# Storing the ranked mask rows seven steps after their gather, from eleven buffers, in a four-layer graph attention kernel

## The chip, the cores and the metric

The kernel runs on one core of a Trainium2 chip. The metric is device time in microseconds (us), the median of several executions. Times inside an execution come from one profiled execution; they are counted from the start of its span.

## What is computed

There are 3,327 nodes with 512 features, a 0/1 adjacency matrix with few ones, and four graph attention layers of 8, 4, 1 and 8 heads. Each layer normalises the features, projects them, and gives every node the softmax-weighted mean of its neighbours' projected rows. The layers follow one another, so no node of a layer can be finished before the rows of its neighbours from the layer before exist:

```python
h = jnp.maximum(_layernorm(x, axis=-1), 0.0)
x = x + _L0_gnn_ref(h, adj, L0_gnn_W, L0_gnn_a_src, L0_gnn_a_dst)
h = jnp.maximum(_layernorm(x, axis=-1), 0.0)
x = x + _L1_gnn_ref(h, adj, L1_gnn_W, L1_gnn_a_l, L1_gnn_a_r)
...
```

Within a layer (here layer 1):

```python
e = jax.nn.leaky_relu(sl[:, :, None] + sr.T[None, :, :], negative_slope=NEG_SLOPE)
e = jnp.where(mask[:, None, :], e, -jnp.inf)
alpha = jnp.nan_to_num(jax.nn.softmax(e, axis=2), nan=0.0)
out = jnp.einsum('nhm,mhd->nhd', alpha, Wh).reshape(n, OUT_DIM)
```

## The kernel before

**Lists.** A first stage turns the adjacency matrix into lists of neighbours and ranks the nodes by how many neighbours they have, so that tile 0 holds the 128 nodes with the longest lists and tile 25 those with the shortest (`CAPS`, from 36 slots down to 11). All of it is 26 tiles of 128 nodes. After that the kernel works in rank order.

**Layers.** A layer reads a table of projected rows in device memory (`tabx` in layer 0, then `tabs[1]` and `tabs[0]` in turn; the page names them all `tab`) and writes the next table. `Tile` handles one tile: `fetch` (line 856) issues from GpSimd (POOL) one indirect gather of 128 rows per list slot, four slots to a buffer `g`; `scored` (875) makes the softmax weights; `group` (897) multiplies the rows with their weights on VectorE (line 916) and adds them up on TensorE (line 921). When a tile's last group is done, `finish` and `ends` (1004, 994) place what follows some steps later: the means, the normalisation, four transposes (450), the projection (468), the scaling of the new rows `v` on ScalarE (475), and the store of the tile's 128 new rows into the next table on SyncE's DMA queue (SP), line 992. In layers 1, 2 and 3 the tiles with the longest lists (one tile, nine tiles, two tiles: `DENSE`) are not gathered but computed as whole masked rows by `Several` and `Wholes`.

**Masks.** The masks for those whole rows are made in layer 0. `Mask` gathers adjacency rows, turns them, and stores the result in `found` by columns in the old node order. `Ranked` (1050) brings them into rank order: for each of the 26 row tiles, its `fetch` gathers 128 rows of 288 int32 from `found` on POOL and stores them into `masks` on SP (line 1060). Between the two the rows lie in one of three buffers inside the tile `spare`. `Ranked`'s `scored`, `group` and `finish` do nothing.

**Order of the work.** Line 1389 runs over the steps of a layer. Each step issues the fetches of steps up to `LOOK` = 7 ahead, then the pieces placed by `later` (335), then the `scored` of the next step and the `group` of this one. In layer 0 the list of steps ends like this (lines 1381 and 1382), with tile 0's groups last among the tiles' and 18 steps that have nothing but a `Ranked`:

```python
steps[-8:] = [s for i, step in enumerate(steps[-8:]) for s in (step, (Ranked(i), 0))]
steps += [(Ranked(j), 0) for j in range(8, NT)]
```

The instructions of POOL, PE, DVE and ACT are issued in exactly the order of the code (`manual_schedule`, line 1339). SP is not in that list: the order of its queue is chosen by the scheduler of the language, which keeps to the data dependencies and may move a transfer of SP ahead of or behind others. Each transfer in the queue waits there for its own semaphores.

**The start of layer 1.** `Several.place` (1317) for tile 0 puts loads of layer 1 at its start: `s` (1221), the first slices of table rows `v` (1243) and of masks (1244), all into the tile `low`. POOL's gathers of layer 1 (834, into `g`, from `tab`) need every row of the new table, so they wait for the last store of line 992, which is tile 0's. The weights of layer 3 are loaded in the same place on SP (393), since the weights of layer 0's projection have had their last reader then.

Of the kernel before, what the change touches and what calls it, by code (L numbers as in the profile page):

```python
# [13 lines left out]
I32 = mybir.dt.int32  # L14
# [4 lines left out]
P = 128  # L19
# [18 lines left out]
ND = max(DENSE)  # L38
# [485 lines left out]
def tile_gat_stack(ctx: ExitStack, tc: tile.TileContext, x, adj, adjT, ws, avs, out):  # L524
# [266 lines left out]
    with cond.Else():  # L791
        tile_gat_lists(tc, x, adj, ws, avs, out, ident, half, slots, L, low, spare, tabx, tabs)
# [3 lines left out]
def tile_gat_lists(ctx: ExitStack, tc: tile.TileContext, x, adj, ws, avs, out, ident, half, slots, L, low, spare, tabx, tabs):  # L796
# [7 lines left out]
    nc = tc.nc  # L804
# [17 lines left out]
    wide = 3 * P  # L822

    found = dram.tile([NP, ND * P // 4], I32, name="found")
    masks = dram.tile([ND // 3, NT, P, wide // 4], I32, name="masks")
# [5 lines left out]
    L, low, spare = [t.rearrange("p a b -> p (a b)") for t in (L, low, spare)]  # L831

    def gather(out_, table, which):
        nc.gpsimd.indirect_dma_start(out=out_, out_offset=None, in_=table,  # L834
                                     in_offset=bass.IndirectOffsetOnAxis(ap=which, axis=0))
# [9 lines left out]
    class Tile:  # L845
# [10 lines left out]
        def fetch(self):  # L856

            l, t = self.l, self.t
            i = len(self.groups)
            k0 = self.k0[i]  # L860
            n = (self.k0 + [CAPS[t]])[i + 1] - k0
            g = gpool.tile([P, GROUP, ROW], F32, name="g")
            for q in range(n):
                if l > 0 and k0 + q == 0:
                    nc.sync.dma_start(g[:, 0, :], tabs[l % 2][t * P:(t + 1) * P, :])
                elif l > 0:
                    gather(g[:, q, :], tabs[l % 2], slots(t, k0 + q))
                elif k0 + q == self.own:
                    gather(g[:, q:q + 2, :].rearrange("p q n -> p (q n)"), tabx, slots(t, 0))
                else:  # L870
                    gather(g[:, q, :], tabx.rearrange("r (s n) -> (r s) n", s=2),
                           slots(t, k0 + q + (k0 == 0), twice=True))
            self.groups.append((k0, n, g))
# [23 lines left out]
        def group(self, i):  # L897


            H, K, wt = HEADS[self.l], CAPS[self.t], self.wt  # L900
            D = F // H
            k0, n, g = self.groups[i]
            if H == 1:
                for q in range(n):
                    v = g[:, q, :].rearrange("p (s m) -> p s m", s=2)[:, :, :F // 2]
                    acc = self.po.rearrange("p (s m) -> p s m", s=2)
                    w = wt[:, k0 + q, 0:1]
                    if k0 + q == 0:
                        nc.vector.tensor_scalar(acc, v, w, None, OP.mult)
                    else:  # L910
                        nc.vector.scalar_tensor_tensor(acc, v, w, acc, OP.mult, OP.add)  # L911
                return
            m = pools["m"].tile([P, GROUP, F], F32, name="m")
            for q in range(n):
                v = g[:, q, :].rearrange("p (s m) -> p s m", s=2)[:, :, :F // 2]
                nc.vector.tensor_tensor(m[:, q, :].rearrange("p (s h d) -> p s h d", s=2, d=D),  # L916
                                        v.rearrange("p s (h d) -> p s h d", d=D),
                                        wt[:, k0 + q, :H].rearrange("p (s h) -> p s h", s=2)
                                        .unsqueeze(3).to_broadcast([P, 2, H // 2, D]), OP.mult)
            for q in range(n):  # L920
                nc.tensor.matmul(self.po, ident, m[:, q, :], start=(k0 + q == 0), stop=(k0 + q == K - 1))  # L921
# [128 lines left out]
    class Ranked:  # L1050
# [3 lines left out]
            self.j, self.k0 = j, [0]  # L1054

        def fetch(self):
            n = ND * P // 4
            rows = spare[:, self.j % 3 * n:(self.j % 3 + 1) * n].bitcast(I32)
            gather(rows, found, slots(self.j, 0))
            nc.sync.dma_start(masks[:, self.j, :, :].rearrange("s p c -> p s c"),  # L1060
                              rows.rearrange("p (s c) -> p s c", c=wide // 4))

        def scored(self, i):
            pass

        group = finish = scored

    class Whole(Tile):

# [275 lines left out]
    for l in range(NL):  # L1345
# [3 lines left out]
        with ExitStack() as c2:  # L1349
# [39 lines left out]
            for s in range(-1, at_end):  # L1389
# [10 lines left out]
                if 0 <= s < len(steps):  # L1400
                    tl, i = steps[s]
# [55 lines left out]
```

## Time and profile before

| | us |
|---|---|
| median of 3 runs | 2471.52 |
| lowest and highest run | 2468.46 and 2473.81 |
| the profiled execution's own time | 3002.17 |
| its span | 3000.4 |
| layer 0's gathers end (last gather into `g`, POOL) | 1070.57 |
| layer 0's last new rows are made (ACT, start of line 475) | 1107.97 |
| layer 1's gathers begin (POOL) | 1117.48 |
| busy: PE, DVE, POOL, ACT | 2240.5, 1911.3, 1749.3, 913.9 |

A profile line of the timeline gives the start, the length, the engine, the line of the code, the operation, and what it writes from what it reads; in brackets stands how long the engine was idle before it and what ended that. SPq and POOLq are the queues in which SyncE and GpSimd issue transfers: the length there is that of the issue, not that of the transfer.

### The profile page before, as it was taken

The numbers are of one execution on the slowest core, as the hardware profiler recorded it, in microseconds if no ns is written. First come the engines' busy times: TensorE is split into PE (matmuls) and PEld (weight loads), VectorE is DVE, ScalarE is ACT, GpSimd is POOL, SyncE is SP. The second block draws the span as 40 slices with busy tenths as digits, with TensorE's granted clock in tenths as the row PEclk, the third lists the DMA queues.
The fourth block names the chain that finished last, engine by engine and source line by source line (L and its number), as shares of the span: only waits on it lengthen the run. The fifth ranks groups of instructions, "written<-read, shape, count | busy, mean of one in ns | idle before, by whom it ended". The sixth has DMA issues, their size and how long they took to land. (4 is left out here: it accounts for less than half of the span.)

```text
span 3000.4 us, 26820 instructions
## 1 busy us (share of the span) xinstructions
PE 2240.5 (75%) x6832; PEld 1225.4 (41%) x6832; DVE 1911.3 (64%) x5004; ACT 913.9 (30%) x2506; POOL 1749.3 (58%) x1739
## 2 busy tenths in 40 slices
PE   4777677777767756778778787679796677888787
PEld 2664243443334333444434344345354343444443
DVE  7887656655555545557665564697887456666655
ACT  5782122322221112323232222343333223332220
POOL 7894455565556646454556562676663556565654
PEclk9888888998899888889988888899898788898988
DMA  6885576786676677666766663787784667676664
GB/s 232 309 294 162 163 221 200 212 253 205 189 206 192 199 186 209 181 177 179 200 183 196 181 186 105 236 247 229 218 253 123 202 187 206 182 202 192 202 171 122
DMA packets 262490, 599.55 MB, mean 200 GB/s; under 512 B 103923, under 2 KB 121331, under 8 KB 257974
## 3 DMA queue, kind: packets, MB, share of 16 engines
q0 software_dynamic: 126128, 438.08, 49.7%
q1 hardware_dynamic: 132454, 152.86, 16.1%
q10 hardware_dynamic: 3744, 6.82, 0.7%
q8 instruction: 55, 0.90, 0.1%
q14 instruction: 109, 0.89, 0.1%
HBM read 547.96 MB, written 49.65 MB: 199 GB/s over the span
## 5 line engine op out<-in xcount | busy, mean ns | idle before, releaser
L921 PE MATMUL bank<-m,ident 128*128 128x512 f32 x2608 | 1328.8, 657 | 376.6 <-DVE m L916 218.1
L916 DVE TENSOR_TENSOR m<-g,pw 128x512 f32<-128x512 f32 x1304 | 811.1, 682 | 539.0 <-ACT pw L890 254.4
L834 POOL DMA_INDIRECT g<-tab,idxb x734 | 698.5, 952 | 482.2 <-issue 200.9
L921 PEld LDWEIGHTS bank<-m,ident 128*128 128x128 f32 x2608 | 528.0, 210 | 1038.3 <-issue 646.6
L468 PE MATMUL pv<-w,hT 128*128 128x264 f32 x1664 | 437.7, 418 | 80.0 <-ACT hT L457 45.5
L834 POOL DMA_INDIRECT g<-tabx,twiceb x342 | 324.2, 948 | 248.4 <-issue 153.7
L834 POOL DMA_INDIRECT g<-tab,idxa x297 | 283.0, 953 | 231.1 <-issue 95.6
L468 PEld LDWEIGHTS pv<-w,hT 128*128 128x128 f32 x1664 | 335.9, 206 | 182.5 <-ACT hT L457 52.3
L890 ACT ACTIVATE pw<-z 128x32 f32<-128x32 f32 (+4 forms) x362 | 69.1, 191 | 801.6 <-DVE z L889 442.5
L1146 PE MATMUL whole<-ve,em 128*128 128x512 f32 x468 | 230.1, 644 | 52.0 <-issue 21.8
L694 POOL TENSOR_TENSOR key<-a,keys 128x3328 int32<-128x3328 int32 (+1 forms) x29 | 189.4, 6534 | 16.2 <-DVE cand L703 12.6
L911 DVE SCALAR_TENSOR_TENSOR bank<-g,L,bank 128x512 f32<-128x512 f32 x243 | 183.3, 754 | 11.8 <-remote 3.9
L1146 PEld LDWEIGHTS whole<-ve,em 128*128 128x128 f32 x468 | 94.2, 207 | 164.7 <-issue 124.3
L834 POOL DMA_INDIRECT g<-tabx,twicea x99 | 94.4, 954 | 105.6 <-issue 55.5
L703 DVE MAX8 cand<-key 128x8 f32<-128x208 int32 x416 | 143.9, 364 | 0.1
L450 PE MATMUL pt<-ident,xn 128*128 128x128 f32 x416 | 71.4, 300 | 95.6 <-ACT xn L966 48.4
L475 ACT ACTIVATE v<-pv,rstd 128x528 f32<-128x528 f32 x78 | 54.1, 694 | 265.9 <-remote 118.6
L1271 ACT ACTIVATE spare<-room,low 128x64 f32<-128x64 f32 x208 | 57.9, 337 | 191.7 <-remote 82.2
L450 PEld LDWEIGHTS pt<-ident,xn 128*128 128x128 f32 x416 | 55.6, 155 | 137.8 <-ACT xn L966 54.9
L887 DVE TENSOR_TENSOR z<-g,pw 128x32 f32<-128x32 f32 (+4 forms) x362 | 63.1, 174 | 73.2 <-DMA g<-tab,idxa 43.3
L457 ACT ACTIVATE hT<-pt 128x512 f32<-128x512 f32 x104 | 61.4, 590 | 153.8 <-remote 85.1
L1260 ACT ACTIVATE r<-low,spare 128x256 f32<-128x256 f32 x208 | 98.9, 476 | 10.2 <-remote 2.3
(180 smaller groups left out, 2189.4 us busy)
## 6 DMA issues: line engine op xcount, KB each, us to landing
a<-in_adj SPq DMA_DIRECT2D x25, 1664.0 KB
tab<-v SPq DMA_DIRECT2D x78, 264.0 KB
ve<-tab SPq DMA_DIRECT2D x78, 264.0 KB
g<-tab SPq DMA_DIRECT2D x66, 264.0 KB
tabx<-vx SPq DMA_DIRECT2D x26, 528.0 KB
g<-tab,idxb POOLq DMA_INDIRECT x734
low<-tab SPq DMA_DIRECT2D x52, 132.0 KB
room<-tab SPq DMA_DIRECT2D x52, 132.0 KB
```

The costliest lines, as they stand in the source:

```text
L450: nc.tensor.transpose(pt[:, k, :], xn[:, k * P:(k + 1) * P], ident)
L468: nc.tensor.matmul(pv[:, s, :HF + 8], hT[:, k, :], W.w[:, k, s, :], start=(k == 0), stop=(k == KC - 1))
L694: nc.gpsimd.tensor_tensor(key[:, c:c + quarter], a[:, c:c + quarter], keys[:, c:c + quarter], OP.mult)
L703: nc.vector.max(cand[:, g * 8:(g + 1) * 8], key[:, g * SEG:(g + 1) * SEG])
L834: nc.gpsimd.indirect_dma_start(out=out_, out_offset=None, in_=table, in_offset=bass.IndirectOffsetOnAxis(ap=which, axis=0))
L887: nc.vector.tensor_tensor(z, g[:, :n, ROW - 8:ROW - 8 + H], self.s.unsqueeze(1).to_broadcast([P, n, H]), OP.add)
L890: nc.scalar.activation(self.wt[:, k0:k0 + n, :H], z, AF.Exp)
L911: nc.vector.scalar_tensor_tensor(acc, v, w, acc, OP.mult, OP.add)
L916: nc.vector.tensor_tensor(m[:, q, :].rearrange("p (s h d) -> p s h d", s=2, d=D), v.rearrange("p s (h d) -> p s h d", d=D), wt[:, k0 + q, ...
L921: nc.tensor.matmul(self.po, ident, m[:, q, :], start=(k0 + q == 0), stop=(k0 + q == K - 1))
L1146: nc.tensor.matmul(tl.po.rearrange("p (s m) -> p s m", s=2), e[:, q * P:(q + 1) * P], v.rearrange("p (s m) -> p s m", s=2)[:, :, :F // 2], ...
L1260: nc.scalar.activation(self.r[:, h, :], self.a[:, g, :], AF.Relu, bias=-1.0, scale=self.b[:, j, g:g + 1])
```

## The change

`Ranked.fetch` only gathers now. The store into `masks` is issued in `Ranked.group`, which the loop calls when the step itself is reached, seven steps (`LOOK`) after its fetch. The rows lie in `low` and no longer in `spare`; `low` has 26 x 128 = 3,328 columns, so `many` is 3328 // 288 = 11 buffers in place of three.

```diff
         def fetch(self):
-            n = ND * P // 4
-            rows = spare[:, self.j % 3 * n:(self.j % 3 + 1) * n].bitcast(I32)
-            gather(rows, found, slots(self.j, 0))
-            nc.sync.dma_start(masks[:, self.j, :, :].rearrange("s p c -> p s c"),
-                              rows.rearrange("p (s c) -> p s c", c=wide // 4))
+            n, many = ND * P // 4, low.shape[1] // (ND * P // 4)
+            i = self.j % many
+            self.rows = low[:, i * n:(i + 1) * n].bitcast(I32)
+            gather(self.rows, found, slots(self.j, 0))
 
         def scored(self, i):
             pass
 
-        group = finish = scored
+        finish = scored
+
+        def group(self, i):
+
+            nc.sync.dma_start(masks[:, self.j, :, :].rearrange("s p c -> p s c"),
+                              self.rows.rearrange("p (s c) -> p s c", c=wide // 4))
```

## Prediction

> **What bounds the kernel now.** I begin with the page: how long the span is, and what the chain of work that ended last consists of.
>
> ```profile
> span 3000.4 us, 26820 instructions
> PE 11%; DVE 7%; issue 7%; POOL 3%; ACT 2%; another core or an unknown queue 2%; DMA 1%; DVEq 0%; POOLq 0%; ACTq 0%
> ```
>
> No engine carries the whole; the four layers run one after another, each on its own mixture of gathers, DVE and PE. The change touches one place, the seam between layer 0 and layer 1. The chain view has no piece there, so I follow it by hand in the timelines, backwards from layer 1's first work. DVE first:
>
> ```profile
> 1104.09 0.15 DVE L885 COPY pw<-g 128x4 f32<-128x4 f32 x1
> 1123.85 0.17 DVE L887 TENSOR_TENSOR z<-g,pw 128x16 f32<-128x16 f32 x1 [19.61 <-DMA g<-tab,idxa]
> ```
>
> DVE has nothing to do for 19.61 us and waits for layer 1's first gathers. POOL issues them:
>
> ```profile
> 1070.57 0.94 POOL L834 DMA_INDIRECT g<-tabx,twiceb  x1 [4.21 <-issue]
> 1071.81 0.95 POOL L834 DMA_INDIRECT spare<-found,idxb  x1 [0.31 <-issue]
> 1073.06 0.95 POOL L834 DMA_INDIRECT spare<-found,idxb  x1 [0.30 <-issue]
> ...
> 1100.94 0.94 POOL L834 DMA_INDIRECT spare<-found,idxa  x1 [1.95 <-DMA masks<-spare]
> 1102.41 0.94 POOL L834 DMA_INDIRECT spare<-found,idxa  x1 [0.53 <-issue]
> 1103.82 0.94 POOL L834 DMA_INDIRECT spare<-found,idxa  x1 [0.46 <-issue]
> 1106.91 0.94 POOL L834 DMA_INDIRECT spare<-found,idxa  x1 [2.15 <-DMA masks<-spare]
> 1108.28 0.94 POOL L834 DMA_INDIRECT spare<-found,idxa  x1 [0.43 <-issue]
> 1117.48 0.94 POOL L834 DMA_INDIRECT g<-tab,idxa  x1 [8.26 <-DMA tab<-v]
> ```
>
> The first one, at 1117.48, waited for the transfer tab<-v, tile 0's new rows. Before it stand the mask gathers: the one of row tile 7 at 1071.81, that of row tile 25 at 1108.28, so 18 intervals in 36.47 us, 2.03 us each. Every third waits for a store of `masks`: three buffers hold them back. Now ACT, which makes the new rows, and SP's queue, which stores them:
>
> ```profile
> 1107.97 0.70 ACT L475 ACTIVATE v<-pv,rstd 128x528 f32<-128x528 f32 x1 [5.32 <-PE pv L468]
> ```
>
> ```profile
> 1110.52 0.39 SPq L1244 DMA_DIRECT2D spare<-masks  x1
> 1111.14 0.36 SPq L1060 DMA_DIRECT2D masks<-spare  x1
> 1111.59 0.44 SPq L393 DMA_DIRECT2D w<-in_w  x1
> 1112.08 0.53 SPq L992 DMA_DIRECT2D tab<-v  x1
> 1112.66 0.42 SPq L393 DMA_DIRECT2D w<-in_w  x1
> 1116.73 0.33 SPq L1221 DMA_DIRECT2D low<-tab  x1
> ```
>
> The rows are ready at 1107.97 + 0.70 = 1108.67, yet their store is issued at 1112.08, 3.41 us later. In front of it in the queue stand the last mask store (1111.14), which had to wait for the gather of 1108.28, and half of layer 3's weights (1111.59). The seam is therefore set by the mask rows, and only just: they end some 3 us after the computation of tile 0, which has run since 1070.57 beside them.
>
> **What the Trainium skill says.** In "DMA: Bandwidth & Descriptors", section "Anatomy of one DMA — SWDGE (gpsimd) path", it says that DMA engines do not wait on semaphores, the wait happens on the issuing sequencer before dispatch. So a store that waits for its gather holds up everything behind it in SP's queue; the 3.41 us agree. The same section prices a transfer at 2.0 us plus bytes / 436e3; for 128 x 288 x 4 = 147,456 bytes that is an estimate of 2.3 us. The trace is longer: 1106.91 to the dependent store at 1109.99 is 3.1 us, and the slowest I found (1075.69 to 1079.81) 4.1 us; I use the trace. The section "Queues, rings and completion order" of that page says that a DMA engine consumes one ring in order, so the rows' transfer also stands behind the weights' bytes issued before it on SP. The trace agrees in one comparison. At the next such seam, from layer 2 to layer 3, no weights go ahead:
>
> ```profile
> 2320.07 0.32 SPq L992 DMA_DIRECT2D tab<-v  x1
> ...
> 2323.18 1.00 POOL L834 DMA_INDIRECT g<-tab,idxa  x1 [9.77 <-issue]
> ```
>
> From the issue of the store to the first gather it is 3.1 us there, and 1117.48 - 1112.08 = 5.4 us here.
>
> **The change part by part.** It removes no instruction and adds none: 26 gathers and 26 stores remain, 147,456 bytes each.
>
> Eleven buffers: gather j now waits for store j - 11 in place of j - 3. Gathers 7 to 25 can follow at the pace of back-to-back issues on POOL, 1071.81 to 1073.06 = 1.25 us. Gather 25 is then issued at 1071.81 + 18 x 1.25 = 1094.3 instead of 1108.28. Its store, 3.1 to 4.1 us later, is issued by 1098.4. The stores of eleven back are long done: gather 22 (1090.6) needs store 11 (gather 1076.8, store by 1080.9, landed at most 3.8 us later, as store 1079.81 released the gather at 1083.62). Bytes: 2 x 147,456 per 1.25 us is 236 GB/s; between 1090 and 1105 the DMA engines moved 151 GB/s at a busy share of 0.56, so about 270 GB/s at full share in this mixture. It fits, at a share near 0.87.
>
> The delay: in the code the last new row would come before the last 13 stores. In the built instruction order of the changed kernel it does not: SP's scheduler puts all 26 stores, then tile 25's own row for layer 1, three mask loads, two table loads and the first half of the weights ahead of it. So the delay as such does nothing for that row; what helps is that the 26 stores end early. Those five loads and the tile's row stood among the stores before; at 0.45 us an issue they take 2.7 us, from 1098.4 to 1101.1. The row's store also has a semaphore wait for the transfer eight back on SP, store 25: landed by 1098.4 + 3.8 = 1102.2. SP is then idle until the weights' buffer and the rows are ready. Slack: 1108.67 - 1102.2 = 6.5 us.
>
> Moved as well: tile 1's row, at 1082.85 before, stands behind store 15 now, some 1085.4 (gather 15 at 1081.8 plus 3.6). Only a table load 15 us later reads it. An early load of layer 3's mask moves up behind store 0 and holds SP until that has landed; before, a mask load of layer 1 did the same at 1029.78. Cost nothing both times, since store 1 was not due before 1033.73. If its gather came sooner, it costs what is missing, 3.8 us at most, with 75 us of cover behind it.
>
> `low` is also layer 1's work space, so its first ACT, DVE and PE instructions, and the loads into it, wait for the mask stores to have read it. All are done by 1102.2, and layer 1's first such writer (L1236) ran at 1120.60. Nothing, as long as the 6.5 us of slack stand. `spare` becomes free earlier; nobody waits for it.
>
> The sum: the rows' store is issued when they are ready, at about 1108.75 instead of 1112.08: 3.3 us. Its way to the first gather took 5.4 us with the weights' first half 0.5 us ahead. In the changed order that half waits for PE alone: at the earliest for the first eight matmuls of the projection, which fill about half of 1102.70 to 1107.93, at the latest for its end at 1107.93. It is ahead by 0.8 to 3.4 us; the 5.4 us become something between 5.4 and 3.1. I take 1.1 us off, half the distance, so 4.4 us in all, 3.3 to 5.6. What is late next is tile 0's own computation (projection and ACT), untouched. After the seam everything hangs on those rows, so the gain is carried to the end: 3002.17 - 4.4 = 2997.8 in the profiled execution.
>
> The timed executions take 2471.52, 0.823 of the profiled one's 3002.17, and I don't know how the two chains that race here (18 mask rounds in 39.3 us, 1071.81 to 1111.14; computation of tile 0 in 38.1 us, 1070.57 to 1108.67) stand there. If both shrink alike, the gain is 4.4 x 0.823 = 3.6 us: 2467.9.
>
> **Rivals.**
> Forecast: 2467.9, 0.15% less. For it speak the waits above; chance 0.50, of which 0.10 beyond 0.2%.
> Hidden: in the timed executions the mask rounds are shorter by more than the computation. 3.4 us of 39.3 are enough, 9%, and SP is free before the rows are ready already; the gain is nil: 2471.5. For it speaks that the profiled execution is slower overall by far more than 9%, against it that nothing shows which of the two shrinks. Chance 0.18, 0.02 of it slower.
> Larger: the computation shrinks more than the rounds. In the profile SP would be free at 1102.2, so 1112.08 - 1102.2 = 9.9 us could be saved, with 1.1 for the weights 11.0, times 0.823 = 9.1: 2462.4 at the end. Midway between this and the forecast: 2465.2. Chance 0.20.
> Slower: the mask traffic does not become faster, because gathers and stores, closer together, slow each other down. Now six transfers, 2.7 us, and the wait for store 25's landing stand between it and the rows. With the old pace of 2.03 us the store is issued at 1111.14, landed at 1114.9: the rows go 2.9 us later, times 0.823 = 2.4: 2473.9. It decides once store 25 is issued after 1112.08 - 3.8 = 1108.3, its gather after 1104.7, a pace over (1104.7 - 1071.8) / 18 = 1.83 us. Against it speaks the DMA share of 0.56. Chance 0.12, of which 0.05 beyond 0.2%.
>
> **How the numbers follow.** A measurement of this kernel can tell about 0.2%, 4.9 us, from no change. Faster: 0.10 + 0.20 = 0.30; slower: 0.02 + 0.05 = 0.07; within: 0.63. The range goes from the larger gain's end, 2462.5, to the slower rival's 2474.
>
> **What would show it.** In the profile of the changed kernel: mask gathers from 1071.8 on 1.25 us apart with no wait for `masks`; the last mask store before 1100; L992's last store within 0.2 us of the end of ACT L475; the first gather from `tab` 4 to 5.6 us earlier relative to that of tile 0's last gather from `tabx`. I am wrong if the mask gathers still stand 1.8 us apart or more, if the store waits for store 25, or if the gap between ACT and the store is gone and the median has not moved.

## The result and the profile after

| | before, us | changed, us |
|---|---|---|
| median of 6 runs | 2470.99 | 2459.62 |
| lowest and highest run | 2468.46 and 2473.81 | 2455.74 and 2461.02 |
| ratio of the changed kernel to the one before, 95% interval | | 0.9951 (0.9940 to 0.9961) |
| the profiled execution's own time and its span | 3002.17 and 3000.4 | 2458.72 and 2456.9 |

The changed kernel takes 11.4 us less. The forecast was 3.6 us less, and 2459.62 lies below the whole range, whose lower end was 2462.5.

The page of the changed kernel, the line with its span:

```profile
span 2456.9 us, 26822 instructions
```

The span is 543.5 us shorter than the 3000.4 of before, while the medians differ by 11.4. The profile of before was one unusually long execution: profiled again, the same kernel took 2467.62 us with a span of 2465.9. The mean clock granted to TensorE was 0.874 in the long execution, and 0.946 and 0.947 in the profiles of after and of before taken again; what made the long one long was not found. From here on the second profile of before is the one to compare with, since it and the profile of after stand for the timed runs.

First the kernel before, profiled again, at the seam between layer 0 and layer 1. POOL's timeline, with the last gather of layer 0, the mask gathers of row tiles 7, 18, 21 and 25, and the first gather of layer 1:

```profile
887.27 0.95 POOL L834 DMA_INDIRECT g<-tabx,twiceb  x1 [0.30 <-issue]
888.52 0.95 POOL L834 DMA_INDIRECT spare<-found,idxb  x1 [0.30 <-issue]
...
914.01 0.94 POOL L834 DMA_INDIRECT spare<-found,idxa  x1 [2.02 <-DMA masks<-spare]
...
919.82 0.95 POOL L834 DMA_INDIRECT spare<-found,idxa  x1 [1.89 <-DMA masks<-spare]
...
927.13 0.94 POOL L834 DMA_INDIRECT spare<-found,idxa  x1 [0.56 <-issue]
...
936.09 0.94 POOL L834 DMA_INDIRECT g<-tab,idxa  x1 [8.02 <-DMA tab<-v]
```

ACT, which makes the new rows, and SP's queue, which stores them, in the same execution:

```profile
908.36 0.70 ACT L475 ACTIVATE v<-pv,rstd 128x528 f32<-128x528 f32 x1 [5.60 <-PE pv L468]
```

```profile
929.97 0.36 SPq L1060 DMA_DIRECT2D masks<-spare  x1
930.42 0.44 SPq L393 DMA_DIRECT2D w<-in_w  x1
930.91 0.53 SPq L992 DMA_DIRECT2D tab<-v  x1
```

The rows are ready at 908.36 + 0.70 = 909.06 and are stored at 930.91, 21.9 us later. In the long execution that gap was 3.4 us. The last mask store, at 929.97, goes out just before it, with only half of the weights between them.

Now the changed kernel, the same three views:

```profile
886.35 0.95 POOL L834 DMA_INDIRECT g<-tabx,twiceb  x1 [0.30 <-issue]
887.60 0.94 POOL L834 DMA_INDIRECT low<-found,idxb  x1 [0.30 <-issue]
...
910.12 0.95 POOL L834 DMA_INDIRECT low<-found,idxa  x1 [0.30 <-issue]
923.54 0.95 POOL L834 DMA_INDIRECT g<-tab,idxa  x1 [12.47 <-DMA tab<-v]
```

```profile
906.12 0.70 ACT L475 ACTIVATE v<-pv,rstd 128x528 f32<-128x528 f32 x1 [5.61 <-PE pv L468]
```

```profile
914.07 0.36 SPq L1069 DMA_DIRECT2D masks<-low  x1
...
917.44 0.38 SPq L393 DMA_DIRECT2D w<-in_w  x1
917.92 0.45 SPq L992 DMA_DIRECT2D tab<-v  x1
```

No mask gather waits for a store any more: the gathers of row tiles 7 to 25 take 910.12 - 887.60 = 22.5 us in place of 927.13 - 888.52 = 38.6 us. But the row is still late. It is ready at 906.82 and stored at 917.92, 11.1 us later, because the last mask store (914.07), six loads (914.52 to 917.34) and half of the weights (917.44) stand before it in SP's queue. So the same thing bounds the seam before and after the change, for less time.

I call "seam" the time from layer 0's last gather to layer 1's first: 936.09 - 887.27 = 48.8 us before, 923.54 - 886.35 = 37.2 us after. It is 11.6 us shorter, and the medians differ by 11.4. The gain is here: in the profiles of all the kernels in this document, the long execution apart, the span without the seam is 2417.1 to 2426.1 us, while the seam goes from 25.5 to 60.5. That the two differences agree within 0.2 us is closer than one execution each can show; the two spans differ by 9.0 us.

The windows view over the time from the first of these mask gathers to the row's store (its columns are the time, the busy time of PE, PEld, DVE, ACT and POOL, the granted clock, the DMA share and GB/s), first before, then after:

```profile
888.50:930.90 42.40, 12.84 (x31) 6.97 (x30) 7.99 (x26) 3.41 (x9) 17.95 (x19) 0.68 0.64 169
```

```profile
887.60:917.90 30.30, 14.47 (x36) 7.58 (x34) 8.07 (x26) 3.40 (x9) 17.98 (x19) 0.78 0.92 241
```

POOL is busy for the same 18 us in both; before, it waited for buffers in between.

### The profile page after: what moved, and what is told of

The parts are those of the page before. It is cut to its first block, busy times and chain, and to the rows that moved or that the text cites. A ratio compares the mean times of both kernels' runs of the same rounds, so it can differ in the third digit from the quotient of the medians.

```text
span 2456.9 us, 26822 instructions
## 1 busy us (share of the span) xinstructions
PE 2082.3 (85%) x6832; PEld 1164.1 (47%) x6832; DVE 1918.9 (78%) x5004; ACT 911.0 (37%) x2506; POOL 1751.1 (71%) x1739
## 5 line engine op out<-in xcount | busy, mean ns | idle before, releaser
L921 PE MATMUL bank<-m,ident 128*128 128x512 f32 x2608 | 1200.8, 606 | 136.3 <-DVE m L916 135.6
L921 PEld LDWEIGHTS bank<-m,ident 128*128 128x128 f32 x2608 | 480.9, 192 | 716.3 <-issue 342.5
L1116 ACT ACTIVATE r<-low,mc,b 128x384 f32<-128x384 f32 x78 | 52.6, 675 | 151.3 <-DVE em L1123 127.8
L889 DVE SCALAR_TENSOR_TENSOR z<-z 128x32 f32<-128x32 f32 (+5 forms) x434 | 86.1, 198 | 15.1 <-DVE z L887 0.2
L431 POOL TENSOR_TENSOR rstd<-ve,half 128x1 f32<-128x1 f32 x52 | 31.9, 614 | 79.7 <-DVE ve L974 42.5
```

Source lines behind the costliest of these rows:

```text
L889: nc.vector.scalar_tensor_tensor(z, z, SLOPE, z, OP.mult, OP.max)
```

## The experiments

The theory after these traces, called A: in a typical execution the computation of tile 0 ends long before the mask rows, the row of tile 0 is held in SP's queue by mask stores that wait for their gathers, and the change gains by the number of buffers alone. The rivals: the delay orders the transfers better; the move from `spare` to `low` helps by itself; or what holds the row is no longer the queue but its own way through busy DMA engines. Where a figure "pace" stands below it is the mean interval of the mask gathers of row tiles 7 to 25, and "rows ready" is the end of ACT's line 475 for tile 0. Nothing of the computation is left out in any of the kernels.

**The kernel before, profiled again.** No edit.

> The kernel before, unchanged, profiled once more. The profile of before that the prediction used came from an execution of 3002 us, the changed kernel's from one of 2459. Theory A (in an execution of the median's length the computation of tile 0 is done long before the mask rows, and the pace of the mask rows alone sets the seam): a span near 2470; mask gathers 7 to 25 about 2.0 us apart as in the long profile; the last new row stored some 20 us after ScalarE has made it; from the last gather into g to the first gather from tab about 47 us, against 37.2 in the changed kernel's profile. Theory B (the seam was much as the long profile showed it, and the gain comes from elsewhere in the kernel): the row stored 3 to 5 us after it is made, and that stretch at most 40 us.

It took 2467.62 us (one run, span 2465.9). Its seam was shown above. SP holds the row for 21.9 us, and not for 3.4 as in the first profile. Why the computation is faster here, and the masks aren't, is seen on DVE. In this execution DVE's work on tile 0's last full group waits for its gather:

```profile
891.25 0.19 DVE L887 TENSOR_TENSOR z<-g,pw 128x32 f32<-128x32 f32 x1 [4.30 <-DMA g<-tabx,twiceb]
```

The same group in the long execution came with no wait for a gather:

```profile
1090.39 0.18 DVE L887 TENSOR_TENSOR z<-g,pw 128x32 f32<-128x32 f32 x1
```

There DVE's group came 1090.39 - 1070.57 = 19.8 us after layer 0's last gather was issued, here 891.25 - 887.27 = 4.0 us. The computation lagged behind its gathers in the long execution, and here it keeps up with them. From this group to the rows being ready it takes about as long in both: 1108.67 - 1090.39 = 18.3 us there, 909.06 - 891.25 = 17.8 us here. The mask gathers show no such lag: in neither profile do those from row tile 7 on wait for DVE, PE or ACT. Why the computation lagged in the long execution stays open.

**Eleven buffers, no delay.** On the kernel before:

```diff
-            rows = spare[:, self.j % 3 * n:(self.j % 3 + 1) * n].bitcast(I32)
+            rows = low[:, self.j % 11 * n:(self.j % 11 + 1) * n].bitcast(I32)
```

> The buffers alone: eleven in low, but the store issued in the fetch as before. Its built order of SP's queue is the changed kernel's, store for store. Theory A: the whole gain, a ratio to before of 0.995 to 0.996. Rival (the delay of seven steps brings the gain): 1.000.

Measured: 2461.41 against 2471.01, ratio 0.9957 (0.9943 to 0.9971). Pace 1.25 us, rows ready 909.12, row stored 919.1, seam 37.6 us, as in the changed kernel (37.2). The order of SP's queue is the same as in the changed kernel, transfer for transfer: the scheduler puts the stores where it puts them, with the delay in the code or without. So the delay is worth nothing here, and the buffers are the whole change. (In the code the delay is six rounds of the loop and not seven: in the round of step s the fetches run to step s + 6.)

**Three buffers, but in `low`.** As above with `% 3`.

> The place alone: the rows in low as in the changed kernel, but three buffers, and the store in the fetch as before. Theory A (the number of buffers sets the pace): no gain, a ratio of 0.999 to 1.001, mask gathers 2.0 us apart. Rival (the gain comes from moving the rows out of spare, which changes the loads that SP puts among the stores): 0.995 to 0.997.

Measured: 2469.90 against 2471.01, ratio 0.9996 (0.9989 to 1.0004). Pace 2.13 us, seam 48.9 us (48.8 before). The place is worth nothing.

**The late stores in ACT's queue.** On the changed kernel, the stores of row tiles 8 to 25 are issued from ACT and no longer stand in SP's queue:

```diff
         def group(self, i):
 
-            nc.sync.dma_start(masks[:, self.j, :, :].rearrange("s p c -> p s c"),
+            queue = nc.scalar if self.j >= 8 else nc.sync
+            queue.dma_start(masks[:, self.j, :, :].rearrange("s p c -> p s c"),
```

> The changed kernel, with the mask stores of row tiles 8 to 25 issued from ScalarE's queue, whose order is that of the code; so tile 0's new row is really ahead of stores 13 to 25, and SP has none of them in front of it. Theory A says that the changed kernel still loses about 11 us between the row (ready at 906.82 in its profile) and its store (917.92) to the mask stores ahead of it: the row is stored within 1 us of being ready, the first gather from tab follows right behind the last mask gather on POOL, some 11 us earlier, ratio to before 0.990 to 0.992. Rival (what bounds the seam now is POOL's mask gathers or the row's own way through the DMA engines, not SP's queue): 0.994 to 0.996, as the changed kernel.

Measured: 2451.88 against 2471.01, ratio 0.9925 (0.9910 to 0.9939), seam 28.9 us. The rows are ready at 908.60, and SP stores them at once:

```profile
908.63 0.32 SPq L992 DMA_DIRECT2D tab<-v  x1
```

On POOL, the gather of row tile 24 and the first of layer 1:

```profile
913.01 0.94 POOL L834 DMA_INDIRECT low<-found,idxa  x1 [4.00 <-DMA masks<-low]
...
915.60 0.95 POOL L834 DMA_INDIRECT g<-tab,idxa  x1 [0.30 <-issue]
```

The wait between ready and stored is 0.03 us; it was 11.1 us. So it was SP's queue that held the row, and nothing in the row itself. The first gather of layer 1 comes 8 us earlier and not 11, as POOL itself now waits 4.00 us: the stores that free its buffers stand behind the activation of `v` in ACT's order (the first of them goes out at 907.96, just after that activation starts). A wait was taken from one queue and a shorter one came up in another.

**Two buffers.** On the kernel before, `% 2` in `spare`.

> The kernel before with two buffers in spare in place of three, all else the same. Theory A (pace = one round of gather, store and landing, shared by the buffers): in the new profile of before a round takes 5.85 us (gathers 908.08, 914.01, 919.82, 925.63), so two buffers give 2.9 us a gather in place of 1.95; 16 or 17 gathers bound by it make the seam 15 to 16 us longer, ratio 1.006 to 1.007. Rival (the seam isn't set by the number of buffers): 1.000.

Measured: 2482.33 against 2472.89, ratio 1.0037 (1.0024 to 1.0051). Pace 2.97 us, seam 60.5 us. The row's store in SP's queue, and the end of the mask gathers on POOL:

```profile
932.29 0.49 SPq L992 DMA_DIRECT2D tab<-v  x1
```

```profile
946.54 0.94 POOL L834 DMA_INDIRECT spare<-found,idxa  x1 [0.53 <-issue]
947.79 0.95 POOL L834 DMA_INDIRECT g<-tab,idxa  x1 [0.30 <-issue]
```

The pace was expected and came; the loss is smaller than expected (11.7 us of seam and 9.4 of the median, where 15 to 16 were expected). In this kernel SP's order is another one: the row goes at 932.29, among the mask stores instead of behind them, and the first gather of layer 1 waits for POOL's own last mask gather only, 1.25 us before it. So the number of buffers sets the pace, as theory A says, but what stands ahead of the row depends on the order that the scheduler chose for that kernel.

**Four buffers in `low`.** `% 4`.

> Four buffers in low, store in the fetch. Theory A: 5.85 / 4 = 1.46 us a gather, still over the 1.25 us of POOL's issue, so the gain is 17 x (1.95 - 1.46) = 8 us, about 0.997; with rounds a little longer in the denser traffic 0.9975. Rival (any buffer beyond three gives the whole gain, or only eleven give it): 0.9955, or 1.000.

Measured: 2467.57 against 2472.89, ratio 0.9976 (0.9967 to 0.9985). Seam 44.7 us, pace 1.90 us. The ratio came as expected, the pace did not. With three buffers, three gathers come every 5.8 us (914.01 to 919.82 above). If a round took as long with four, the pace would be 5.8 / 4 = 1.46 us. It takes longer: the gathers of every fourth row tile start at 896.80, 903.22, 910.11, 918.23 and 925.57, so a round is 6.4 to 8.1 us. The transfers take longer: for row tiles 14 to 25 the store follows its gather by 2.9 to 4.0 us here and by 2.8 to 3.3 with three buffers, and a store's landing reaches 3.7 us in place of 2.2 (medians 2.2 and 2.0), while the DMA share over these gathers is 0.76 in place of 0.64. So the gain of a buffer is less than its share. That the denser traffic makes them slower fits these numbers, but was not tested by itself; and the profile is that of the longest of the 17 executions (2472.67 us). At eleven the issue on POOL, 0.95 + 0.30 = 1.25 us, is the limit.

**The stores in ACT's queue, one step earlier.** On the changed kernel. The step's `scored` is called ahead of the `group` of the step before, so ACT issues the stores ahead of `v`, and POOL's wait should go:

```diff
         def scored(self, i):
+            if self.j >= 8:
+                self.store(nc.scalar)
+
+        def group(self, i):
+            if self.j < 8:
+                self.store(nc.sync)
+
+        def finish(self, s):
             pass
 
-        finish = scored
-
-        def group(self, i):
-
-            nc.sync.dma_start(masks[:, self.j, :, :].rearrange("s p c -> p s c"),
-                              self.rows.rearrange("p (s c) -> p s c", c=wide // 4))
+        def store(self, queue):
+            queue.dma_start(masks[:, self.j, :, :].rearrange("s p c -> p s c"),
+                            self.rows.rearrange("p (s c) -> p s c", c=wide // 4))
```

> Late mask stores on ScalarE's queue as before, but each one step earlier (in scored), so that stores 13 and 14 stand ahead of ScalarE's scaling of tile 0's new rows and not behind it. In the run without this, mask gathers 24 and 25 waited for them (4.00 us at 913.01). Theory A: that wait is gone, the mask gathers end about 4 us earlier, and the first gather from tab follows when the row has landed, 3 to 4 us earlier; ratio to before 0.9905 to 0.9915. Rival (the row's own landing bounds it by then): 0.992 to 0.993, unchanged.

Measured: 2450.28 against 2472.89, ratio 0.9899 (0.9880 to 0.9917). POOL's wait for buffers is gone (pace 1.25 us, the last mask gather at 912.78), and the seam is the same, 28.7 us against 28.9:

```profile
910.71 0.32 SPq L992 DMA_DIRECT2D tab<-v  x1
```

```profile
917.75 0.94 POOL L834 DMA_INDIRECT g<-tab,idxa  x1 [4.03 <-DMA tab<-v]
```

The row is stored at 910.71, 0.02 us after it is ready, and its way from there to the first gather is 917.75 - 910.71 = 7.0 us. From 910 to 918 the DMA share is 0.99 at 315 GB/s. By the trace the rival is right: once nothing holds the row in the queue, its own landing bounds the seam. The ratio does not decide it: it lies below both expected ranges, its interval overlaps that of the late stores' run (0.9910 to 0.9939), and the two were measured beside different runs of before.

**The weights in ACT's queue.** On the changed kernel, both halves of layer 3's weights (512 KB each), of which SP issues the first 0.5 us before the row and the second 0.5 us after it, go to ACT:

```diff
-                nc.sync.dma_start(self.w[:, :, s, :HF],
+                (nc.scalar if l == 3 else nc.sync).dma_start(self.w[:, :, s, :HF],
```

> The changed kernel with layer 3's weights loaded from ScalarE's queue inside layer 1, so that none of their bytes go ahead of tile 0's row at the seam. The prediction's term for them: the row's way from issue to the first gather, 5.6 us in the changed kernel (917.92 to 923.54), becomes 3 to 4 us, as at the seam from layer 2 to 3 (3.1 us); 1.5 to 2.5 us less, ratio to before 0.994 to 0.995. Rival (the mask bytes still under way, not the weights, make it 5.6 us): unchanged, 5.4 to 5.8 us and 0.995 to 0.996.

Measured: 2457.16 against 2472.89, ratio 0.9929 (0.9911 to 0.9947). Seam 34.5 us. SP's row and POOL's first gather:

```profile
921.44 0.38 SPq L992 DMA_DIRECT2D tab<-v  x1
```

```profile
924.77 0.94 POOL L834 DMA_INDIRECT g<-tab,idxa  x1 [9.75 <-DMA tab<-v]
```

The row's way is 3.3 us, against 5.6 us in the changed kernel (917.92 to 923.54). ACT issues the weights at 1011.6 and 1012.0, long after the seam, so none of their bytes move beside the row any more. In the seven profiles in which the row goes out between the two halves and behind all the mask stores, its way is 5.2 to 6.2 us. The two halves together cost some 2.3 us; what the one ahead and the one behind cost singly was not tested. The ratio does not show this gain: it lies below both expected ranges, and the changed kernel itself has 0.9951 beside one set of runs of before and 0.9931 beside another.

**Both.** The last two edits together.

> Late mask stores on ScalarE's queue one step earlier, and layer 3's weights on ScalarE's queue inside layer 1. In the run with the first alone the row's way from issue to the first gather was 7.0 us (910.71 to 917.75), with the second alone 3.3 (921.44 to 924.77). Theory A, with the weights' bytes as the cause: about 4 to 5 us, the seam from the last gather of layer 0 to the first of layer 1 becomes 26 us in place of 28.7, bounded then by POOL's last mask gather; ratio to before 0.988 to 0.990. Rival (the mask bytes on the way are the cause of the 7.0 us): 28 to 29 us and no gain over the run without, 0.990 to 0.992.

Measured: 2449.28 against 2473.13, ratio 0.9908 (0.9893 to 0.9923). Rows ready 906.10, row stored 906.12; then the last mask gather and the first of layer 1 on POOL:

```profile
906.12 0.32 SPq L992 DMA_DIRECT2D tab<-v  x1
```

```profile
909.33 0.95 POOL L834 DMA_INDIRECT low<-found,idxa  x1 [0.30 <-issue]
911.08 0.95 POOL L834 DMA_INDIRECT g<-tab,idxa  x1 [0.80 <-DMA tab<-v]
```

The seam is 25.5 us, 23.3 shorter than before, and the median is 23.9 us shorter. The row's way is 5.0 us: mask stores go out beside it on ACT's queue, and the DMA share from 906 to 911 is 1.00, where it was 0.49 from 921 to 925 in the run with the 3.3 us. The first gather stands 1.75 us behind POOL's last mask gather, where 1.25 is the least seen. Little is left between them. That the weights' move still gains on top of the stores' is seen in the seam alone (28.7 to 25.5 us, in one execution each, this one the shortest of its four); the ratios 0.9899 and 0.9908 have overlapping intervals and don't show it, and 0.9908 lies in the range of the rival.

**The changed kernel again,** measured on the same chip and beside the same runs of before as the last one. No edit.

> The changed kernel, unchanged, on the same chip as the run above, to compare with: 0.995 to before, a seam of 37 us, the row's store 11 us after it is ready.

Measured: 2456.47 against 2473.13, ratio 0.9931 (0.9918 to 0.9945), pace 1.25 us, row ready 907.71 and stored 920.51, 12.8 us later, seam 37.8 us. Pace and seam are nearly those of the first time (1.25 and 37.2 us), but the gain is 16.7 us where it was 11.4. The medians thus carry some 5 us that the seam does not explain, and ratios that differ by 0.2% are compared only between kernels that share their runs of before. Beside the same runs of before, the kernel with both edits is 7.2 us below the changed one; their seams differ by 12.3 us, in the shortest execution of the one and the longest of the other.

## Why the prediction was wrong

**The step that failed** is the last of the sum: "If both shrink alike, the gain is 4.4 x 0.823 = 3.6 us". The prediction had no ground for that "if"; it said that it didn't know how the chains stand in the timed runs. They don't shrink alike. From layer 0's last gather to the rows being ready it was 38.1 us in the long execution, and 909.06 - 887.27 = 21.8 us in a typical one, 0.57 of it. From the mask gather of row tile 7 to the last mask store it was 39.3 us, and 929.97 - 888.52 = 41.5 us, no shorter at all. Nearly all of the 16.3 us by which the first is shorter are the lag of DVE behind its gathers, 19.8 us in the long execution and 4.0 in a typical one; the 18 us of work after it stayed. The second chain is a ring of gather, landing, store, landing, which waits for no DVE, PE or ACT in these traces, so it had no such lag to lose. The prediction saw the rows held by the masks "only just", for 3.4 us; in a typical execution they are held for 21.9 us. So there was more to gain than the 3.3 us that the prediction gave to the store of the rows: it was 12.1 us, as worked out next.

**The rival "Larger"** had this mechanism: "the computation shrinks more than the rounds". Its limit was too small, 11.0 x 0.823 = 9.1 us. With the rows ready long before their store, how early SP is free decides alone. The mask gathers took 38.6 us before and 22.5 after, 16.1 us less. The row's store follows the last mask gather by 930.91 - 927.13 = 3.8 us before and by 917.92 - 910.12 = 7.8 us after, because six transfers now stand between the last mask store and the row, and that store is 1.1 us further from its gather (2.84 and 3.95 us). So 16.1 - 4.0 = 12.1 us were gained at the row's store; 0.4 of them were lost on its way, and 11.6 are left for the seam. The rival had 9.9 at the store, and 36.5 us in place of 38.6 for the old gathers. Without the factor 0.823, which this ring doesn't follow, its 11.0 us would have been near the measured 11.4, but in part by luck: the 1.1 us for the weights in it did not come, and the slower old gathers made up for them.

**The mask chain's own steps were right.** Pace 1.25 us; the last gather 3.95 us before its store (914.07 - 910.12; 3.1 to 4.1 was taken); six transfers in 917.34 - 914.52 = 2.8 us (2.7 was taken). The buffer of eleven back was free every time. The DMA share is 0.92 at 241 GB/s (0.87 and 236 were worked out). Tile 1's row goes out at 902.19 behind store 15, where it was 901.68 before, and no gather on POOL waited for it.

**The slack did not exist.** "Slack: 1108.67 - 1102.2 = 6.5 us" has the sign turned: SP comes 11.1 us after the rows. So "the rows' store is issued when they are ready" and "L992's last store within 0.2 us of the end of ACT L475" failed too. They came true only with the mask stores out of SP's queue (0.03 us).

**The weights' term** was 1.1 us off the row's way, on the ground that the weights' half would wait for PE alone and go well ahead. With SP late it went 917.92 - 917.44 = 0.48 us ahead, as before, and the row's way became 5.62 us from 5.18. The price of the weights was about right (5.4 us with them and 3.1 without): with both halves taken away, the way is 3.3 us.

**The delay** did nothing, as the built order had said, and the stores kept their place ahead of the row. **The rival "Slower"** needed a pace over 1.83 us; eleven buffers have 1.25. **The rival "Hidden"** expected the mask rounds to shrink more than the computation; the opposite came.

That the long execution was far above the timed runs was seen in the prediction (3002.17 against 2471.52), and its answer was to scale everything by one factor. The factor belongs to no single chain, and here the sum depended on the difference between two.

## What to carry to other kernels

Where two chains race to one point, look at what each consists of before scaling a profile to the timed runs: here the chain that lagged on engines took 0.57 of its time in a typical execution and the ring of transfers 1.05. A profile far above the median should be taken again first. A ring of few buffers filled by a gather and emptied by a store is limited by the round of both transfers; here two, three, four and eleven buffers gave a gather every 2.97, 2.15, 1.90 and 1.25 us. More buffers helped until the issue was the limit, and the round itself got longer meanwhile. A transfer that stands behind such a ring in the same queue waits for all of it: giving the ring another queue than the one that carries the next stage's row gained 9.5 us beyond the buffers here (2461.41 to 2451.88).

## What the runs showed of the hardware

- In the stretch of the seam the landing of a mask store, issued from SP, took 2.0 us at the median before (2.0 to 2.2, DMA share 0.64) and 3.3 us after (2.6 to 3.4, share 0.92). The mask gathers, of the same 147,456 bytes and issued from POOL, took 3.0 to 3.1 us at the median before and 3.8 after. The Trainium skill's "DMA: Bandwidth & Descriptors", section "Anatomy of one DMA — SWDGE (gpsimd) path", fits the path of the gathers without naming a load; its estimate for them is 2.3 us, and both measurements lie above it.
- The way of tile 0's rows (264 KB) from its issue to the gather that needs it went from 3.3 us to 7.0 us, by what moved around it: 3.3 with neither weights nor mask rows, 5.6 with 512 KB of weights just ahead and as much just behind, 5.0 with mask rows beside it, 7.0 with both, in one execution each.
- One execution of the kernel before took 3002 us where its other executions on record take 2464.59 to 2480.93. Its vector, scalar and GpSimd instructions and the issue of its gathers were as long as in the other profile (682 and 683 ns for line 916, 952 ns for a gather), the matmuls of line 921 took 657 ns in place of 607, the mean granted clock was 0.874 in place of 0.947, and the waits between engines were longer. Its cause stays open.
